# A new table of issue times for a fused conv, Fourier-attention and feed-forward kernel on one core

## The chip, the core and the metric

The kernel runs on one core of a Trainium2 chip. A core has a matrix engine (TensorE, PE in the profile; its weight loads are shown apart as PEld), a vector engine (VectorE, DVE), a scalar engine (ScalarE, ACT), a general engine (GpSimd, POOL) and a queue engine (SyncE, SP) that here only issues DMA transfers. Each works through its own list of instructions in order, and they wait for each other by semaphores. SBUF is the working memory, PSUM the memory that TensorE writes its products to[...].

The metric is the time of one execution on the device in microseconds (us), lower being better.

## What is computed

The input is x of 64 images, 96 channels, 56 x 56 pixels, in float32. Two layers follow each other:

```python
# layer 0: inverted bottleneck with squeeze and excitation
out = silu(bn(conv1x1(x, 96 -> 192)))
out = channel_shuffle(shift_groups(out))            # by one pixel up, left, down, right
out = silu(bn(bn(depthwise3x3(out)) + bn(out * id_w)))
se  = sigmoid(grouped(relu(grouped(mean(out)))))    # one gate per channel
x   = silu(bn(conv1x1(out * se, 192 -> 96)) + x)

# layer 1: tokens t of 3136 pixels x 96 channels
def attn(t):                                        # a Fourier filter over the tokens
    X  = fft(relu(bn(t @ w1.T)), axis=1, norm='ortho')
    xr = relu(X.real * diag(r) - X.imag * diag(i) + rb)
    xi = relu(X.imag * diag(r) + X.real * diag(i) + ib)
    return bn(ifft(xr + 1j * xi).real @ w2.T)
t = t + attn(ln(t))
t = t + qlinear(relu(qlinear(ln(t), W1, b1)), W2, b2)   # inputs and weights rounded to fp8 e5m2, sums to fp16
```

## The kernel before

The work of an image is cut into 56 kinds of steps, most of them in several pieces: 7 pieces of x to load, 7 ea_mm steps and so on. A step is a Python function that issues a few instructions on one engine. There is no loop over images with a body: line 42 holds PERIOD and line 43 a table PLAN with one number for every piece of every kind, and at the end of the kernel one sort puts all pieces of all 64 images in one order:

```python
for _, b, k, i in sorted(
    (b * PERIOD + when, b, k, i)
    for b in range(NB)
    for k, step in enumerate(STEPS)
    for i, when in enumerate(PLAN[step.__name__])
):
    STEPS[k](b, i)
```

The numbers are only sort keys: nothing on the chip looks at a time. What they settle is the order in which each engine's instructions are issued, and with it which image's pieces stand between which others, and the order in which buffers are taken from their pools. About four images are in work at a time. While image b has its depthwise product, image b-1 has its Fourier product, and image b-2 its feed-forward part. Waits on data, on buffers and on shared PSUM banks are put in by the framework, following that order.

In the order of one image, with the engine and the line that the profile shows:

- **x_in** (SP, L175): 7 pieces of 8 image rows into the single buffer `xi`, two transfers of 48 channels each. A piece may overwrite its rows once the `pj_add` steps of the image before have read them.
- **ea_mm, eb_mm** (PE, L383, L400) with **ea_ev, eb_ev** (ACT, L388, L413): the expanding 1x1 product with the shift built into the window, 128 channels in `e_a` and 64 in `e_b`.
- **dw_mm** (PE, L446) with **dw_ev** (ACT, L456): the depthwise product of the 128 channels as 32 x 32 diagonal products, in two halves of three steps of 96 products each. A half takes all four tiles of the pool `psb`; steps 0 to 2 are the first, 3 to 5 the second half. dw_ev 0 to 3 and 4 to 7 read the tiles out.
- **lt** (DVE, L466 and L468) and **ls** (ACT, L471): the nine taps of the other 64 channels, and their silu.
- **se1, se2** (PE, ACT, DVE), ending in se2_pw (DVE, L517), which makes the gated projection weight `pw`.
- **pj_mm** (PE, L532, L537), **pj_add** (DVE, L543), **pj_ev** (ACT, L549): the projection in two halves, the addition of x, and the silu into one of three buffers `t`.
- **c_mm, c_sq, c_v, c_pow, sp** (PE, ACT, DVE, POOL): the first layernorm's sums. sp_ev ends with a small transfer on SP (L612).
- **w1_mm, w1_ev** (PE L626, DVE L638); **f1_mm, f1_ev** (PE L653, ACT L665); **f2_mm** (PE L680, L690): the attention's first product and the Fourier transform in two stages. f2_mm has six groups of frequency rows, each in one tile of `psa`, of which there are two; a tile takes two PSUM banks.
- For each f2 group i: **f2_u** 2i and 2i+1 (ACT, L705) read the tile's first 56 columns per row into the two halves of `ue`; **f2_s** 2i and 2i+1 (DVE, L721 and L724) read its other 56 columns and each half of `ue`, two instructions per step; **f2_r** i (ACT, L728) and **f2_p** i (DVE, L734) make the filtered values.
- **w2_mm, w2_ev** (PE L745 and L757, ACT L775); **i1_mm, i1_ev** (PE L786, ACT L797); **i2_mm, i2_ev** (PE L808, DVE L821): output product and inverse transform. All of w2, i1, i2, w1, f1 and f2 take turns at the two `psa` tiles. i1_mm has three steps of 128 products of 56 columns each; the first two stand next to each other behind pj_mm 3, which belongs to the next image.
- **n, x_mm, x_ev** (PE, ACT, DVE, POOL), then **h_mm, h_ev, h_b, h_q** (PE L865, ACT L870, DVE L875, ACT L881), 21 steps each, and **o_mm, o_ev, o_b, o_f, o_st** (PE L887, ACT L892, DVE L897, POOL L903, SP L909), 7 each: the second layernorm, the quantized feed-forward part, the last addition and the store.

The pool `psb` has four tiles of one PSUM bank and hands them out in turn, so a step that takes a tile waits for the one that took it four tiles ago to be read out. The order on PE around the depthwise product of image b is, before the change: f2 1 and 0 (of b-1), dw 0, 1, 2 (of b), f2 2, h 6, h 8, h 7 (of b-2), f2 3, dw 3, 4, 5, f2 4, h 9, o 1, se1, f2 5, h 10, se2, h 12, h 11, w2 0, w2 1, and then pj 0 of b.

## Time and profile before

| | us |
|---|---|
| median of 3 runs | 7470.06 |
| lowest and highest | 7461.43, 7473.81 |
| the profiled execution | 7463.64 |
| its span, first to last instruction | 7461.9 |
| busy: PE, DVE, ACT, POOL | 7176.9, 4829.5, 4654.4, 1513.6 |
| granted TensorE clock | 0.991 |

The span is 1.7 us short of the profiled execution's own time. The costliest groups on PE are the depthwise product (1033.2 us busy, 36864 products of 498 ns, which overlap), the Fourier product f1 (688.9), w1 (676.2), ea (429.6) and eb (415.3). On DVE it is the taps of the 64 channels (971.5, 512 of 1898 ns), on ACT the 1344 casts h_q (739.0) and the 1344 casts h_ev (697.2). DMA engines are busy about a tenth of the time.

Busy times are sums over overlapping work, and the end of a product on PE is modelled; so start times are the better measure of PE's progress. "issue" as the releaser of a wait means that the engine waited for nothing that the profile shows.

### The profile page before, as it was taken

How to read it: one execution, taken by the hardware profiler on the slowest of the kernel's cores; microseconds unless marked ns; L12 is line 12 of the kernel's file. 1: busy time of each engine (PE TensorE's matmuls, PEld its weight loads, DVE VectorE, ACT ScalarE, POOL GpSimd, SP SyncE). 2: the span in 40 equal slices, each digit the busy share in tenths (PEclk: the TensorE clock that was granted, in tenths of full speed). 3: DMA queues.
4: the chain of work that ended last, by engine and by line, in shares of the span. 5: the costliest groups of instructions: out<-in, count | busy, mean ns of one | idle time of the engine just before them, and what ended most of it. 6: DMA issues, size and time to landing. Idle time of an engine off the chain costs nothing.

```text
span 7461.9 us, 383252 instructions
## 1 busy us (share of the span) xinstructions
PE 7176.9 (96%) x177666; PEld 5259.2 (70%) x177666; DVE 4829.5 (65%) x8795; ACT 4654.4 (62%) x9806; POOL 1513.6 (20%) x1360
## 2 busy tenths in 40 slices
PE   7999999999999999999999999999999999999997
PEld 4777777777777776777777777777777777777775
DVE  5666666666666666666666666666666666666664
ACT  3566666666665666656656666666566566665665
POOL 0221212212212122122121221221212212212112
PEclk9999999999999999999999999999999999999998
DMA  1010110110101101101011011010110110101100
GB/s 48 20 27 18 29 27 19 29 24 21 28 17 29 27 19 28 24 22 28 17 29 27 19 28 25 22 28 18 29 27 19 29 26 20 29 21 26 28 20 21
DMA packets 424331, 185.32 MB, mean 25 GB/s; under 512 B 378785, under 2 KB 422041, under 8 KB 422473
## 3 DMA queue, kind: packets, MB, share of 16 engines
q1 hardware_dynamic: 420970, 155.82, 9.1%
q8 instruction: 1392, 22.81, 1.3%
q10 hardware_dynamic: 1264, 3.48, 0.1%
q14 instruction: 209, 1.71, 0.1%
q0 software_dynamic: 496, 1.50, 0.1%
HBM read 82.80 MB, written 77.07 MB: 21 GB/s over the span
## 4 chain that ended last, share of the span: by engine, by line
PE 85%; ACT 6%; DVE 6%; issue 3%; DMA 0%; POOL 0%; POOLq 0%; SPq 0%; ACTq 0%
PE psa L653 9%; PE psa L626 9%; PE ps_d L446 8%; PE ps_eb L400 5%; PE ps_ea L383 5%; PE psa L808 5%; PE ps_pj L532 5%; PE ps_c L557 5%; PE psa L745 5%; PE ps_n L557 5%; PE psa L786 5%; PE psa L680 4%; PE ps_h L865 4%; PE ps_o L887 3%; DVE s L721 3%
## 5 line engine op out<-in xcount | busy, mean ns | idle before, releaser
L903 POOL TENSOR_TENSOR o<-t,o 112x448 f32<-112x448 f32 x448 | 613.9, 1370 | 3694.7 <-DMA out_dram<-o 1710.0
L446 PE MATMUL ps_d<-e_a,diag 32*32 32x392 f32 x36864 | 1033.2, 498 | 0.7 <-ACT d L456 0.7
L468 DVE SCALAR_TENSOR_TENSOR d_last<-e_b,taps,d_last 128x1568 f32<-128x1568 f32 x512 | 971.5, 1898 | 7.1
L875 DVE TENSOR_SCALAR y<-y,qb 128x448 f16<-128x448 f16 x1344 | 479.8, 365 | 683.9 <-ACT y L870 676.7
L568 DVE TENSOR_REDUCE v<-sq 112x4 f32<-112x384 f32 x896 | 491.3, 548 | 662.7 <-ACT sq L564 662.1
L446 PEld LDWEIGHTS ps_d<-e_a,diag 32*32 32x32 f32 x36864 | 673.6, 103 | 288.9 <-issue 40.0
L870 ACT CAST y<-ps_h 128x448 f16<-128x448 f32 x1344 | 697.2, 540 | 213.1 <-PE ps_h L865 209.5
L837 POOL TENSOR_TENSOR rs<-v,mhalf 112x4 f32<-112x4 f32 x448 | 490.3, 1099 | 1453.9 <-DVE v L569 1453.9
L881 ACT CAST h<-y 128x448 fp8e5<-128x448 f16 x1344 | 739.0, 571 | 3.0 <-DVE y L875 3.0
L653 PEld LDWEIGHTS psa<-f_tab,buf_h 128*56 128x56 f32 x24576 | 655.4, 131 | 77.8 <-DVE v L569 42.5
L626 PEld LDWEIGHTS psa<-w1c,t 112*64 112x64 f32 x14336 | 604.0, 137 | 141.4 <-DVE v L569 45.4
L653 PE MATMUL psa<-f_tab,buf_h 128*56 128x58 f32 x24576 | 688.9, 216 | 0.0
L626 PE MATMUL psa<-w1c,t 112*64 112x96 f32 x14336 | 676.2, 249 | 2.9 <-DMA t<-dev_t 1.4
L586 POOL TENSOR_TENSOR rs<-v,mhalf 112x4 f32<-112x4 f32 x448 | 447.6, 1012 | 763.6 <-DVE v L569 763.5
L638 DVE SCALAR_TENSOR_TENSOR buf_h<-psa,rs_full 128x768 f32<-128x768 f32 (+1 forms) x512 | 435.4, 851 | 137.4 <-PE psa L626 129.5
L543 DVE TENSOR_TENSOR ps_pj<-ps_pj,x 112x392 f32<-112x392 f32 x512 | 260.6, 566 | 404.5 <-PE ps_pj L537 392.3
L728 ACT ACTIVATE s<-s 128x896 f32<-128x896 f32 (+2 forms) x384 | 334.4, 887 | 288.8 <-DVE s L721 288.8
L388 ACT ACTIVATE e_a<-ps_ea 128x448 f32<-128x448 f32 x448 | 244.9, 547 | 412.5 <-PE ps_ea L383 412.5
L564 ACT ACTIVATE sq<-ps_n 112x384 f32<-112x384 f32 x448 | 214.1, 495 | 436.1 <-PE ps_n L557 434.8
L734 DVE SCALAR_TENSOR_TENSOR buf_h<-ue,s 128x448 f32<-128x448 f32 (+2 forms) x768 | 406.8, 580 | 109.4 <-ACT s L728 109.4
L549 ACT ACTIVATE t<-ps_pj,pjbn_b 112x392 f32<-112x392 f32 x512 | 281.4, 620 | 284.5 <-DVE ps_pj L543 284.5
L786 PE MATMUL psa<-inv_tab,buf_g 112*32 112x56 f32 x24576 | 350.5, 214 | 110.5 <-issue 108.8
(175 smaller groups left out, 13024.5 us busy)
## 6 DMA issues: line engine op xcount, KB each, us to landing
x<-in_x SPq DMA_DIRECT2D x896, 84.0 KB, 3.2
out_dram<-o SPq DMA_DIRECT2D x896, 84.0 KB, 2.2
l_tab<-in_tab_l ACTq DMA_DIRECT2D x1, 1624.0 KB
r_tab<-in_tab_r ACTq DMA_DIRECT2D x1, 1568.0 KB
t<-dev_t SPq DMA_DIRECT2D x64, 7.0 KB, 2.1
t<-dev_t SPq DMA_DIRECT2D x64, 5.2 KB
ex_row_p<-in_expand_row POOLq DMA_DIRECT2D x1, 336.0 KB, 4.5
s_p<-in_bn POOLq DMA_DIRECT2D x1, 288.0 KB, 3.8
```

What stands on the lines that cost most here:

```text
L446: nc.tensor.matmul(pss[r][j * 32 : j * 32 + 32], lhsT=diag[pr, tap, :], rhs=e_a[pr, r0 : r0 + PJ, dx : dx + HW], start=tap == 0, stop=tap ...
L468: nc.vector.scalar_tensor_tensor(d_last, win, w, d_last, ALU.mult, ALU.add)
L557: nc.tensor.matmul(cen[c0:c1, k, 0:C], lhsT=t_of(b)[:, n0 + c0 : n0 + c1], rhs=center, start=True, stop=True)
L568: nc.vector.tensor_reduce(v, sq, AX.X, ALU.add)
L626: nc.tensor.matmul(ps[hc * 64 : hc * 64 + 64, k, 0:C], lhsT=t[:, n0 : n0 + 64], rhs=w1c[:, hc * C : hc * C + C], start=True, stop=True,)
L653: nc.tensor.matmul(ps[r * 64 : r * 64 + HW, k, 0 : 2 * NK], lhsT=buf_h[:, n0 : n0 + HW], rhs=f_tab[:, r, :], start=True, stop=True,)
L786: nc.tensor.matmul(ps[p0 : p0 + 32, k, 0:HW], lhsT=u_v[:, oh * 48 + o, :], rhs=inv_tab[:, r, :], start=True, stop=True,)
L837: nc.gpsimd.tensor_tensor(rs, held.pop(("nv", b, g)), mhalf[0:CP, 0:4], ALU.pow)
L870: nc.scalar.copy(y16, held.pop(("h", b, i)))
L875: nc.vector.tensor_scalar(y16, y16, qb1[:, i % 3 : i % 3 + 1], 0.0, ALU.add, ALU.max)
L881: nc.scalar.copy(held["h8", b, j][:, m, :], held.pop(("y", b, i)), saturate=False)
L903: nc.gpsimd.tensor_tensor(o32, rows, o16, ALU.add)
```

## The change

Every number of PLAN and PERIOD (116.056, then 116.315) is replaced. No step function, no buffer and no other line differs: the same pieces with the same instructions are issued in another order. The rows of the diff that the prediction speaks of:

```diff
-    "x_in": (-142.751, -132.334, -138.890, -139.641, -151.208, -133.652, -137.370),
+    "x_in": (-162.051, -141.566, -142.305, -147.704, -149.731, -127.852, -144.579),
-    "dw_ev": (-67.184, -68.088, -65.354, -62.005, -53.949, -53.481, -53.376, -53.432),
+    "dw_ev": (-75.276, -74.363, -73.773, -71.247, -63.274, -62.310, -61.437, -59.461),
-    "ls": (-56.957,),
+    "ls": (-63.791,),
-    "c_mm": (-24.403, -20.404, -19.123, -17.297, -18.726, -9.644, -8.872),
+    "c_mm": (-31.436, -30.770, -31.175, -30.095, -27.535, -26.998, -26.407),
-    "f2_u": (39.991, 41.910, 38.664, 38.665, 56.185, 56.316, 56.071, 58.643, 62.858, 62.962, 66.464, 67.055),
-    "f2_s": (42.369, 43.646, 41.684, 42.524, 58.496, 59.412, 59.011, 59.603, 66.349, 66.780, 67.365, 69.133),
-    "f2_r": (44.699, 46.227, 59.499, 60.966, 71.228, 72.985),
-    "f2_p": (46.153, 47.154, 60.124, 60.967, 72.402, 74.345),
+    "f2_u": (36.232, 37.748, 35.978, 39.758, 48.352, 51.224, 45.857, 47.326, 55.183, 57.358, 59.477, 63.260),
+    "f2_s": (40.754, 40.796, 41.011, 41.830, 49.823, 52.099, 45.858, 50.177, 56.136, 57.359, 62.673, 66.022),
+    "f2_r": (40.797, 43.254, 52.791, 53.034, 64.718, 69.300),
+    "f2_p": (44.390, 44.463, 53.286, 53.767, 68.705, 72.198),
-    "i1_mm": (82.811, 83.639, 91.924),
+    "i1_mm": (78.634, 79.503, 87.989),
```

On PE the order stays close to what it was. Around the depthwise product it is now f2 0, h 3, f2 1, dw 0, 1, 2, f2 3, h 7, h 8, h 6, f2 2, dw 3, 4, 5, f2 4, f2 5, h 9, o 1, se1, h 10, se2, h 12, h 11, w2 0, w2 1, pj 0. The order on ACT between dw_ev 0 and w2_ev 0, before and after (h and o steps are of image b-2, dw, ls and se steps of b, f2 and w2 of b-1):

```
before: dw_ev 1, 0, 2, h_ev 6, 8, dw_ev 3, h_ev 7, f2_u 6, 4, h_q 6, f2_u 5, 7, ls, f2_r 2, 3, dw_ev 4, 5, 7, 6,
        f2_u 8, 9, se1_ev, o_ev 1, h_ev 9, h_q 8, f2_u 10, 11, h_q 7, h_ev 11, se2_th, h_ev 10, w2_ev 0
after:  dw_ev 0, 1, 2, f2_r 1, h_ev 6, 8, dw_ev 3, h_ev 7, f2_u 6, 7, 4, 5, h_q 6, 8, ls, f2_r 2, 3, dw_ev 4, 5, 6,
        f2_u 8, dw_ev 7, h_ev 9, f2_u 9, se1_ev, o_ev 1, f2_u 10, h_ev 10, f2_u 11, h_q 7, f2_r 4, h_ev 11, h_q 9,
        se2_th, w2_ev 0
```

On DVE the f2_s steps of the second pair of groups change from 4, 6, 5, 7 to 6, 4, 7, 5. On SP the order per image changes from x 4, o_st 5, o_st 0, x 0, 3, 2, 6, o_st 2, x 5, 1, o_st 1 to x 0, o_st 0, x 4, 3, 6, 2, 1, o_st 1, o_st 4, sp_ev 0, x 5, where the stores belong to an image three before that of the loads (o_st 5 and 0 of the old order to two other ones).

More of the change, by code (lines that the diff above doesn't have):

```diff
@@ L38 @@
 AT = {k: i for i, k in enumerate(ROWS)}
-PERIOD = 116.056
+PERIOD = 116.315
 PLAN = {
-    "x_in": (-142.751, -132.334, -138.890, -139.641, -151.208, -133.652, -137.370),
-    "ea_mm": (-127.116, -124.446, -119.920, -94.498, -104.745, -112.167, -106.964),
-    "ea_ev": (-125.252, -124.279, -119.721, -94.105, -94.974, -110.456, -105.960),
-    "eb_mm": (-110.852, -109.364, -102.468, -94.672, -100.705),
-    "eb_ev": (-109.889, -108.508, -98.175, -94.671, -100.704),
-    "dw_mm": (-77.186, -75.415, -71.686, -59.708, -58.836, -58.630),
-    "dw_ev": (-67.184, -68.088, -65.354, -62.005, -53.949, -53.481, -53.376, -53.432),
-    "lt": (-93.236, -91.843, -90.397, -86.333, -83.176, -78.618, -75.060, -71.072, -58.358),
-    "ls": (-56.957,),
-    "se1_mm": (-52.674,),
-    "se1_ev": (-52.590,),
-    "se2_mm": (-49.560,),
-    "se2_ev": (-47.764,),
-    "se2_th": (-46.882,),
-    "se2_pw": (-44.842,),
-    "pj_mm": (-44.604, -44.263, -36.259, -33.499),
-    "pj_add": (-41.623, -41.337, -40.573, -40.255, -32.468, -30.814, -32.509, -32.127),
-    "pj_ev": (-41.036, -40.637, -40.429, -36.736, -30.334, -29.230, -31.146, -29.797),
-    "c_mm": (-24.403, -20.404, -19.123, -17.297, -18.726, -9.644, -8.872),
-    "c_sq": (-23.198, -19.663, -17.391, -16.366, -11.963, -8.651, -8.871),
-    "c_v": (-21.831, -17.939, -17.390, -11.021, -10.842, -8.366, -8.657),
-    "c_pow": (-19.058, -12.292, -10.931, -8.952, -1.526, -3.948, -1.526),
-    "sp_v": (-8.951, -1.525),
-    "sp_mm": (-6.057, 0.802),
-    "sp_ev": (-5.461, 1.113),
-    "w1_mm": (1.423, -2.619, 3.588, 18.203, 8.943, 12.171, 13.999, 16.535),
-    "w1_ev": (3.273, -0.045, 7.600, 20.920, 11.591, 14.999, 15.957, 19.212),
-    "f1_mm": (21.608, 26.248, 24.638, 31.810, 32.559, 32.004),
-    "f1_ev": (25.169, 25.895, 30.841, 28.844, 27.556, 26.595, 32.009, 32.411, 36.910, 36.732, 36.699, 35.929),
-    "f2_mm": (37.220, 36.994, 44.528, 54.196, 60.721, 63.959),
-    "f2_u": (39.991, 41.910, 38.664, 38.665, 56.185, 56.316, 56.071, 58.643, 62.858, 62.962, 66.464, 67.055),
-    "f2_s": (42.369, 43.646, 41.684, 42.524, 58.496, 59.412, 59.011, 59.603, 66.349, 66.780, 67.365, 69.133),
-    "f2_r": (44.699, 46.227, 59.499, 60.966, 71.228, 72.985),
-    "f2_p": (46.153, 47.154, 60.124, 60.967, 72.402, 74.345),
-    "w2_mm": (70.359, 71.061, 73.352, 79.154),
-    "w2_ev": (70.421, 73.788, 79.483, 82.773),
-    "i1_mm": (82.811, 83.639, 91.924),
-    "i1_ev": (86.931, 93.317, 99.344),
-    "i2_mm": (102.107, 101.737, 110.644, 111.766),
-    "i2_ev": (106.004, 107.037, 104.651, 104.395, 113.248, 110.645, 115.503, 113.393),
-    "n_mm": (109.042, 108.523, 116.336, 120.505, 126.604, 126.539, 137.374),
-    "n_sq": (109.105, 109.021, 116.337, 120.506, 127.174, 126.540, 137.375),
-    "n_v": (109.642, 109.022, 116.338, 120.507, 127.975, 126.902, 138.122),
-    "n_pow": (110.809, 110.170, 116.496, 122.658, 132.126, 129.135, 139.318),
-    "n_x": (112.520, 110.693, 119.248, 123.053, 133.298, 130.929, 139.362),
-    "x_mm": (113.125, 114.113, 121.321, 126.216, 135.244, 138.382, 142.002),
-    "x_ev": (114.896, 115.709, 126.025, 126.217, 137.926, 142.365, 142.302),
@@ new lines @@
+    "x_in": (-162.051, -141.566, -142.305, -147.704, -149.731, -127.852, -144.579),
+    "ea_mm": (-137.812, -138.766, -127.145, -89.430, -97.733, -111.642, -106.253),
+    "ea_ev": (-135.094, -135.727, -126.517, -84.394, -93.721, -111.545, -104.661),
+    "eb_mm": (-115.802, -120.129, -109.842, -102.415, -108.473),
+    "eb_ev": (-111.833, -116.221, -108.303, -102.404, -105.700),
+    "dw_mm": (-76.334, -76.333, -76.332, -65.377, -64.292, -64.065),
+    "dw_ev": (-75.276, -74.363, -73.773, -71.247, -63.274, -62.310, -61.437, -59.461),
@@ new lines @@
+    "lt": (-98.494, -96.392, -95.603, -88.519, -87.554, -85.563, -82.511, -76.163, -74.006),
+    "ls": (-63.791,),
+    "se1_mm": (-59.375,),
+    "se1_ev": (-58.823,),
+    "se2_mm": (-58.487,),
+    "se2_ev": (-51.685,),
+    "se2_th": (-49.080,),
+    "se2_pw": (-49.031,),
+    "pj_mm": (-46.907, -46.770, -39.776, -38.214),
+    "pj_add": (-46.414, -46.480, -46.303, -45.926, -36.420, -35.642, -35.383, -35.834),
+    "pj_ev": (-44.579, -44.088, -42.412, -41.675, -36.419, -34.237, -33.877, -33.743),
@@ new lines @@
+    "c_mm": (-31.436, -30.770, -31.175, -30.095, -27.535, -26.998, -26.407),
+    "c_sq": (-30.893, -30.081, -28.190, -27.946, -25.511, -26.729, -24.086),
+    "c_v": (-30.249, -28.487, -27.216, -25.783, -23.070, -24.232, -21.605),
+    "c_pow": (-28.779, -21.220, -25.415, -24.356, -20.189, -23.395, -9.184),
+    "sp_v": (-20.657, -9.105),
+    "sp_mm": (-16.179, -7.327),
+    "sp_ev": (-14.695, -0.897),
+    "w1_mm": (0.527, -6.007, -2.422, 8.757, 3.678, 7.621, 13.788, 13.807),
+    "w1_ev": (4.695, -0.847, -2.421, 11.306, 5.010, 10.078, 15.828, 14.929),
@@ new lines @@
+    "f1_mm": (20.887, 18.211, 16.353, 22.113, 25.063, 24.097),
+    "f1_ev": (22.512, 22.072, 20.634, 20.909, 16.354, 19.684, 23.039, 23.663, 29.327, 28.458, 27.295, 25.063),
+    "f2_mm": (31.295, 32.252, 47.080, 41.210, 52.876, 55.792),
+    "f2_u": (36.232, 37.748, 35.978, 39.758, 48.352, 51.224, 45.857, 47.326, 55.183, 57.358, 59.477, 63.260),
+    "f2_s": (40.754, 40.796, 41.011, 41.830, 49.823, 52.099, 45.858, 50.177, 56.136, 57.359, 62.673, 66.022),
+    "f2_r": (40.797, 43.254, 52.791, 53.034, 64.718, 69.300),
@@ new lines @@
+    "f2_p": (44.390, 44.463, 53.286, 53.767, 68.705, 72.198),
+    "w2_mm": (65.362, 69.052, 70.502, 74.617),
+    "w2_ev": (67.901, 69.923, 78.367, 78.466),
+    "i1_mm": (78.634, 79.503, 87.989),
+    "i1_ev": (85.994, 87.591, 88.690),
+    "i2_mm": (93.044, 93.367, 101.562, 100.521),
+    "i2_ev": (96.799, 93.389, 96.982, 100.266, 111.406, 109.631, 107.480, 103.660),
+    "n_mm": (96.952, 99.575, 108.486, 116.587, 121.041, 122.075, 127.209),
+    "n_sq": (99.791, 100.349, 108.487, 117.309, 121.042, 122.726, 128.090),
@@ L91 @@
+    "n_v": (101.981, 103.127, 109.950, 117.332, 122.940, 123.624, 129.985),
+    "n_pow": (101.982, 103.583, 112.829, 119.179, 122.941, 123.625, 129.986),
+    "n_x": (105.486, 105.615, 113.313, 120.038, 125.778, 125.828, 132.761),
+    "x_mm": (106.100, 106.737, 115.863, 120.681, 125.990, 132.998, 133.784),
+    "x_ev": (106.881, 107.368, 115.976, 121.004, 126.865, 132.999, 134.355),
     "h_mm": (
-        144.408, 144.539, 142.955, 151.653, 146.123, 151.741, 165.593, 167.081, 167.021, 179.037, 181.701, 184.163,
@@ L93 @@
-        183.315, 191.401, 194.122, 202.572, 203.025, 214.978, 205.482, 214.132, 209.133,
+        136.544, 135.201, 136.984, 147.819, 144.613, 140.473, 159.661, 157.770, 158.449, 172.175, 173.774, 178.994,
+        177.277, 189.872, 189.465, 197.605, 199.164, 206.608, 200.687, 210.643, 205.066,
     ),
     "h_ev": (
-        146.457, 147.163, 146.728, 153.132, 153.156, 154.262, 168.465, 171.753, 169.119, 180.037, 185.733, 184.280,
-        187.040, 192.972, 195.243, 203.531, 205.107, 216.376, 208.878, 222.205, 212.052,
+        137.275, 137.145, 138.242, 147.961, 147.833, 147.527, 159.834, 162.046, 160.395, 173.266, 179.005, 181.613,
@@ L98 @@
+        184.463, 191.247, 191.928, 199.351, 199.788, 208.901, 200.878, 212.968, 205.403,
     ),
     "h_b": (
-        146.899, 148.834, 148.614, 154.505, 157.941, 159.836, 170.515, 176.287, 174.097, 185.812, 187.639, 185.918,
-        191.781, 195.030, 198.861, 204.123, 206.545, 220.428, 209.152, 226.370, 218.475,
+        137.276, 141.744, 141.117, 153.242, 154.679, 148.788, 161.282, 173.396, 162.133, 182.903, 186.070, 184.378,
+        188.999, 195.975, 191.954, 201.844, 202.120, 210.978, 202.978, 215.917, 208.435,
@@ L102 @@
     ),
     "h_q": (
-        149.384, 151.139, 150.029, 159.215, 163.340, 163.159, 172.257, 183.329, 182.397, 187.024, 188.763, 189.403,
-        196.328, 198.478, 200.406, 208.755, 210.002, 221.499, 217.314, 229.791, 224.579,
-    ),
-    "o_mm": (153.028, 179.101, 192.712, 203.850, 207.474, 223.800, 230.382),
-    "o_ev": (154.015, 179.621, 193.552, 207.958, 209.955, 223.824, 232.254),
-    "o_b": (167.276, 193.254, 201.506, 209.696, 210.604, 235.187, 237.499),
-    "o_f": (171.766, 199.519, 206.356, 219.602, 231.322, 259.139, 253.186),
@@ L111 @@
-    "o_st": (197.792, 218.616, 214.282, 229.895, 257.122, 313.688, 263.438),
+        140.919, 141.749, 144.251, 155.904, 156.312, 156.480, 168.059, 179.758, 168.312, 182.908, 186.075, 186.567,
+        191.342, 197.228, 195.477, 205.150, 206.001, 211.207, 209.270, 222.571, 223.802,
+    ),
+    "o_mm": (146.182, 172.743, 190.451, 200.773, 200.074, 212.764, 232.857),
+    "o_ev": (146.312, 174.620, 191.421, 200.998, 200.479, 216.027, 234.615),
+    "o_b": (153.419, 184.679, 196.437, 223.964, 201.880, 232.421, 251.929),
@@ L112 @@
+    "o_f": (177.091, 191.561, 197.796, 234.593, 212.317, 240.011, 266.796),
+    "o_st": (192.867, 211.246, 229.825, 253.850, 214.262, 288.749, 273.012),
 }
```

## The prediction

> **What bounds the kernel now.** I read the head of the page, then the waits, then one period of the timeline on PE, ACT, DVE and SP.

> ```profile
> span 7461.9 us, 383252 instructions
> PE 7176.9 (96%) x177666; PEld 5259.2 (70%) x177666; DVE 4829.5 (65%) x8795; ACT 4654.4 (62%) x9806; POOL 1513.6 (20%) x1360
> q8 instruction: 1392, 22.81, 1.3%
> ```
> PE is busy 96% of the span. The other engines are a third idle over a period, so they matter only where PE waits for one of them. The third line is the fetch of a program: 1392 pieces of 16 KB, [...]which is what PE's 355,332 products and weight loads need: 21.75 per image.

> From one dw step 0 to the next (the first product on L446) the median is 114.5 us. The two PE waits that repeat per image:

> ```profile
> PE psa L786 <- issue: 108.8, 68, 2.2
> PE psa L745 <- DVE ue L724: 50.8, 64, 1.7
> ```
> The first (L786 = i1_mm) names no releaser, the second is w2 step 0 waiting for the second half of f2_s. The timeline of image 26's depthwise stage shows the second one, and the order that the change rearranges (start, duration, engine, line):

> ```profile
> 3016.07 1.75 PE L680 MATMUL psa<-l_tab,buf_g 128*64 128x112 f32 x32
> 3017.76 7.98 PE L446 MATMUL ps_d<-e_a,diag 32*32 32x392 f32 x288
> 3025.66 1.56 PE L690 MATMUL psa<-l_tab,buf_g 128*64 128x112 f32 x28
> 3031.92 1.29 PE L745 MATMUL psa<-w2a,buf_h 128*64 128x96 f32 x26 [0.83 <-DVE ue L724]
> ...
> 3017.23 0.54 ACT L870 CAST y<-ps_h 128x448 f16<-128x448 f32 x1
> 3017.88 1.34 ACT L705 ACTIVATE ue<-psa,fa 128x448 f32<-128x448 f32 x2
> 3019.56 1.35 ACT L705 ACTIVATE ue<-psa,fa 128x448 f32<-128x448 f32 x2
> 3020.79 1.61 ACT L471 ACTIVATE d_last<-d_last,mid_b 128x1568 f32<-128x1568 f32 x1
> 3024.98 0.95 ACT L728 ACTIVATE s<-s 128x896 f32<-128x896 f32 x1 [0.36 <-DVE s L721]
> 3025.84 0.57 ACT L456 ACTIVATE d<-ps_d,mid_b 128x392 f32<-128x392 f32 x1
> ...
> 3020.33 0.68 DVE L721 SCALAR_TENSOR_TENSOR s<-psa,fa,ue 128x448 f32<-128x448 f32 x1 [0.89 <-ACT ue L705]
> 3029.38 0.62 DVE L721 SCALAR_TENSOR_TENSOR s<-psa,fb,ue 128x392 f32<-128x392 f32 x1 [1.33 <-ACT ue L705]
> 3031.24 0.63 DVE L724 SCALAR_TENSOR_TENSOR ue<-psa,fb,ue 128x392 f32<-128x392 f32 x1
> ```
> Three things to see. ACT ends h_ev 7 (L870) at 3017.77, and dw step 3 on PE, begun at 3017.76, has its fourth product 53 ns later: no slack. ACT takes up dw_ev 4 (L456) at 3025.84, where the last product of dw ended at 3025.73: no slack either. And DVE starts the f2_s of a group only when *both* f2_u of that group are done (33 ns after the second ends, though the first ended 0.6 to 1.1 us earlier and DVE stands idle), although a half reads only its own half of ue.

> [...]

> **The change part by part.** Only the order of issue changes. Sorting both tables gives the same 106 PE steps per image. I count from dw step 0 = 0 (3005.84 before), with start-to-start times of the trace: f2_u 0.62 (0.56 for 7 rows, 0.48 for 5), a pair on f2_s 1.32 (1.40 to its end), f2_r 0.86, dw_ev 0.57, ls 1.60, h_ev 0.43, h_q 0.46, f2_p 1.1.

> *1. f2_r 1 before h_ev 6 on ACT.* The new ACT order after dw step 2 is dw_ev 0, 1, 2, f2_r 1, h_ev 6, 8, dw_ev 3, h_ev 7. Before, f2_r 1 came ahead of the dw_ev. dw step 2 ends at 7.94, f2_r 1 starts 1.72 later and holds 0.86, so h_ev 6 starts at 10.52 (before 9.96) and h_ev 7 ends at 12.49. The four tiles of dw step 3 take the PSUM slots of dw_ev 3 and the three h_ev, so its products go on at 12.55 instead of 11.99: **+0.56**. dw step 5 ends at 20.46.

> *2. f2_u and f2_s interleaved.* Before, every f2_u was issued ahead of its group's f2_s. Now the order for the second pair of groups is u6, s6, u7, u4, s4, s7, u5, s5, and for the last two u8, s8, u9, s9 and u10, s10, u11, s11. [...] ACT takes its work in order, so everything behind waits too:
> - u6 12.38 to 13.08, s6 13.11 to 14.51, u7 14.56, u4 15.18 to 15.90, s4 15.93 to 17.33, u5 17.38; s7 and s5 run on to 19.97.
> - behind u5: h_q 6 18.00, h_q 8 18.46, ls 18.92, f2_r 2 20.52, f2_r 3 21.38, and only then dw_ev 4 at 22.24. dw was over at 20.46: ACT is 1.7 us late, where it was 0.1 late.
> - dw_ev 4, 5, 6, then u8 23.95 to 24.64 (now before dw_ev 7, which saves 0.57), s8 to 25.96, u9 26.01 to 26.70, s9 to 28.02. w2 step 0 needs the buffer: 28.07, before 26.08: **+1.99** including the 0.56.
> - se1_ev, o_ev 1, u10 27.13, s10 to 28.97, u11 29.02 to 29.60, s11 to 30.67. w2 step 1 starts at 30.72, before 28.36. The gate's pw (se2_th 31.6, se2_pw to 32.6) is still ahead of pj step 0 at 32.99, before 30.63: **+2.36** from here on.

> PE has nothing else to do there: its products between dw and w2 (f2 4 and 5, h, o, se) take 5.3 us and are all issued ahead of w2.

> *3. pj to i1.* f2_p 5 now stands behind pj_add on DVE. pj_add ends 39.4, f2_p 5 40.2, w2 step 3 is wanted at 40.8; h 14, h 13 and o 2 come ahead of it and o 2 waits 0.1 for pj_ev 2. **+0.1**.

> *4. Gaps between kinds of steps on PE.* The trace gives every kind of change the same gap each time: from the last product of ea to any other kind 0.47 us, eb 0.42 (0.14 after its small step), h 0.28 to 0.29, o 0.28, w1 or n or c 0.18, to its own kind 0.03 to 0.2. Counting both orders (c to c 3 then 5, w1 to ea 2 then 0, x to x 0 then 2, h to w2 2 then 1, and so on), the new order saves 0.20 us per image. 0.13 of it lies before the w2 wait and is lost there: **-0.07**.

> *5. Loads of x.* A stall in i1 comes where two fetches follow within 1.7 us; the resumed product lies 3.2 to 4.3 us (median 3.6) after the previous block's first. All stalls of this kind (each step's time above its quickest tenth over images 8 to 55: i1, and the c and o steps behind it) are 3.4 us per image. x pieces 3, 2 and 6 are issued 0.7 to 2.7 us after i1 begins:

> ```profile
> 3050.79 0.31 SPq L175 DMA_DIRECT2D x<-in_x  x1
> ...
> 7293.28 0.79 PE L786 MATMUL psa<-inv_tab,buf_g 112*32 112x56 f32 x45 [1.35 <-issue]
> ```
> The second line is image 62, at whose i1 no x is left to load (the last x is issued at 7183.3): it stalls 1.35 on this page, against 2.08 for image 25. So most of the stall isn't the loads. On SP the order becomes x 0, o_st 0, x 4, 3, 6, 2, 1: x 3 is now behind the last pj_add of its rows and fires about 2.3 us after i1 begins instead of 0.7. These are 14 loads as before, they only move past o_st 2 and sp_ev 0; x 1 still lands some 9 us before ea step 1, x 5 some 3 us before eb step 1. I take **-0.2**; bounds: 0, if the fetch doesn't feel them, and -0.6, if every stall fell to 3.2.

> The rest (c steps ahead of i1 step 2, w1, n, x, f1) I followed step by step in the same way: each finds its slot and its input 0.3 us or more before PE asks. The tightest are w1_ev 6 before f1, and f1_ev 8 before f2 step 0 (0.4 and 0.6).

> Sum: 2.36 + 0.1 - 0.07 - 0.2 = 2.2 us per image. It acts in the 63 periods in which one image's dw meets the f2 of the one before: +138 us on the profiled execution's 7463.6, 7602. The median shown lies 6 above that execution, so I say 7605. Filling and draining I leave as they are (63 periods of 114.5 leave about 250 us for both; their chains have the same steps).

> **The rivals.** *(a) The waits run one way only*: a f2_u needn't wait for the f2_s in front of it. Then ls is done by 17.4 and ACT is ready when dw ends. Part 1 stays (+0.56), w2 step 0 gains 0.3 and step 1 gives it back: +0.6 + 0.1 - 0.27, about +25 us, 7490. For it: before never issues an f2_u behind an f2_s of its group, so the trace doesn't show the reverse wait. Against it: the 33 ns rule holds in all three groups in which DVE stood waiting[...].
> *(b) Faster, by the fetch*: place L786 and the c and o steps behind it, price at most 0.6 per image by fewer collisions plus 0.2 of gaps, 0.8 x 63 = 50 us, 7415. It decides only if the dw stage costs under 0.8 per image, that is if (a) holds and the slot wait of part 1 is hidden as well. For it: the stalls are the largest wait. Against it: image 62.
> *(c) The loads don't move*: SP sends when pj_add lets it, whatever the table says. Then -0.2 becomes 0: 7618.
> *(d) The lateness compounds*: ACT, late by 1.7, also delays pj_ev and the h chain, another 0.7 per image: 7650.

> **How the numbers follow.** Forecast with (c), 7560 to 7640: 0.67. (d): 0.10. (a): 0.12, a third of it within 0.2%. (b): 0.11. The range that leaves out two tenths reaches from 7530 to 7655. A measurement of this kernel tells about 0.2% (15 us) from no change: faster 0.11, same 0.05, slower 0.84.

> **What would show it.** Right: f2_u 7 and f2_u 5 start just after an f2_s ends; dw_ev 4 starts 1.5 us or more after the last product of dw; the wait on L745 grows from 0.8 to about 2 us per image and a wait appears inside dw step 3 (some 0.6 us); the period is near 116.7. Wrong: f2_u 7 starting beside s6, an L745 wait that shrinks, or an L786 stall well below 1 us.

## The result and the profile after

The new table is slower: 7650.10 us (median of 4 runs, 7645.42 to 7655.18) beside 7465.75 for the kernel before (4 runs), a ratio of 1.0246 with a 95% interval of 1.0228 to 1.0264. That is 184 us, or 2.93 us for each of the 63 periods. The profiled execution took 7655.18 us.

The head of its page, and the waits on PE (in all, times, longest, us):

```profile
span 7653.4 us, 383102 instructions
PE 7322.0 (96%) x177666; PEld 5365.9 (70%) x177666; DVE 4895.7 (64%) x8795; ACT 4669.8 (61%) x9806; POOL 1722.1 (23%) x1360
```
```profile
PE psa L786 <- issue: 100.6, 81, 2.0
PE ps_se L493 <- ACT red L485: 66.6, 64, 1.3
...
PE ps_se L478 <- ACT d L456: 35.9, 67, 0.9
...
PE psa L745 <- DVE ue L724: 0.6, 1, 0.6
```
PE executes the same instructions and is busy 145 us longer (7322.0 beside 7176.9): its products themselves got slower somewhere. The granted clock fell from 0.991 to 0.974. The wait on L745 (w2), 50.8 us before, is gone; in its place PE waits in se1 (L478) and se2 (L493), which stand ahead of w2 in PE's queue and want dw_ev 7 and se1_ev from a late ACT. A reader who looks only at L745 would think that w2 no longer waits.

Image 26, the same stretch as in the prediction (start, duration; dw step 0 is at 3077.58):

```profile
3089.88 0.78 ACT L705 ACTIVATE ue<-psa,fa 128x448 f32<-128x448 f32 x1
3092.13 1.34 ACT L705 ACTIVATE ue<-psa,fa 128x448 f32<-128x448 f32 x2 [1.47 <-DVE ue L724]
3094.94 0.72 ACT L705 ACTIVATE ue<-psa,fa 128x448 f32<-128x448 f32 x1 [1.47 <-DVE ue L724]
3095.57 1.02 ACT L881 CAST h<-y 128x448 fp8e5<-128x448 f16 x2
3096.49 1.60 ACT L471 ACTIVATE d_last<-d_last,mid_b 128x1568 f32<-128x1568 f32 x1
...
3099.77 0.57 ACT L456 ACTIVATE d<-ps_d,mid_b 128x392 f32<-128x392 f32 x1
...
3091.41 0.68 DVE L724 SCALAR_TENSOR_TENSOR ue<-psa,fa,ue 128x448 f32<-128x448 f32 x1
...
3094.22 0.69 DVE L724 SCALAR_TENSOR_TENSOR ue<-psa,fa,ue 128x448 f32<-128x448 f32 x1
...
3098.23 1.56 PE L690 MATMUL psa<-l_tab,buf_g 128*64 128x112 f32 x28
...
3105.54 1.53 PE L745 MATMUL psa<-w2a,buf_h 128*64 128x96 f32 x32
...
3110.57 2.90 PE L532 MATMUL ps_pj<-d,pw 32*112 32x392 f32 x32
```
f2_u 7 starts 14.55 us after dw step 0, 40 ns after f2_s 6 ended at 3092.09, and f2_u 5 at 17.36, 30 ns after f2_s 4: here an f2_u waits for the f2_s in front of it. The prediction counts on that; it was an estimate of mine, which no trace had shown. dw_ev 4 starts at 22.19 where dw was over at 20.7, w2 step 0 at 27.96 and pj step 0 (L532) at 32.99. The prediction had 14.56, 17.38, 22.24, 28.07 and 32.99.

Image 26 is one of the few whose w2 runs at its usual speed; image 25 is the commoner kind. Its PE timeline, and the clock in three stretches of it (stretch, length, busy and count of PE, PEld, DVE, ACT, POOL, PEclk, DMA):

```profile
2983.21 0.36 PE L865 MATMUL ps_h<-xq,q 96*128 96x448 fp8e5 x1
2984.62 0.60 PE L493 MATMUL ps_se<-red,ep_w 24*32 24x1 f32 x32 [1.05 <-ACT red L485]
...
2986.32 2.82 PE L745 MATMUL psa<-w2a,buf_h 128*64 128x96 f32 x32
2989.08 1.55 PE L757 MATMUL psa<-w2b,buf_h 64*64 64x96 f32 x32
2990.56 1.57 PE L745 MATMUL psa<-w2a,buf_h 128*64 128x96 f32 x32
```
```profile
2980.40:2983.80 3.40, 2.38 (x31) 1.26 (x25) 2.48 (x6) 3.04 (x11) 0.00 (x0) 1.00 0.00 0
2983.80:2990.60 6.80, 5.98 (x104) 4.77 (x104) 4.70 (x12) 4.87 (x11) 0.00 (x0) 0.50 0.01 2
2990.60:2994.00 3.40, 3.40 (x83) 2.75 (x84) 2.45 (x4) 2.71 (x5) 1.98 (x1) 0.99 0.03 5
```
The same 32 products of w2 take 2.82 us here and 1.53 in image 26 and in step 1. For 6.8 us the clock is at 0.50, and the fall comes in the pause itself, before se2 (L493) starts. In 57 of the 60 images 2 to 61, w2 step 0 runs in this slow way, each time at the lower clock; before the change, in none. I had not foreseen it.

### The profile page after: what moved, and what is told of

It reads as the page before. It is cut to its first block, busy times and chain, and to the rows that moved or that the text cites. A ratio compares the mean times of both kernels' runs of the same rounds, so it can differ in the third digit from the quotient of the medians.

```text
span 7653.4 us, 383102 instructions
## 1 busy us (share of the span) xinstructions
PE 7322.0 (96%) x177666; PEld 5365.9 (70%) x177666; DVE 4895.7 (64%) x8795; ACT 4669.8 (61%) x9806; POOL 1722.1 (23%) x1360
## 4 chain that ended last, share of the span: by engine, by line
PE 81%; ACT 12%; DVE 4%; issue 2%; DMA 0%; POOL 0%; POOLq 0%; SPq 0%; DVEq 0%; ACTq 0%
PE psa L653 9%; PE psa L626 8%; PE ps_d L446 7%; PE psa L745 5%; PE ps_ea L383 5%; PE ps_eb L400 5%; PE psa L808 5%; PE ps_pj L532 5%; PE psa L786 4%; PE ps_n L557 4%; PE ps_c L557 4%; PE ps_h L865 4%; ACT d L456 3%; PE ps_o L887 3%; ACT ue L705 3%; PE psa L757 3%
## 5 line engine op out<-in xcount | busy, mean ns | idle before, releaser
L903 POOL TENSOR_TENSOR o<-t,o 112x448 f32<-112x448 f32 x448 | 823.0, 1837 | 3756.1 <-DVE o L897 3140.0
L446 PE MATMUL ps_d<-e_a,diag 32*32 32x392 f32 x36864 | 1062.6, 498 | 0.8 <-ACT d L456 0.7
L468 DVE SCALAR_TENSOR_TENSOR d_last<-e_b,taps,d_last 128x1568 f32<-128x1568 f32 x512 | 1003.2, 1959 | 7.1
L446 PEld LDWEIGHTS ps_d<-e_a,diag 32*32 32x32 f32 x36864 | 698.9, 103 | 293.5 <-issue 26.7
L875 DVE TENSOR_SCALAR y<-y,qb 128x448 f16<-128x448 f16 x1344 | 497.4, 382 | 634.1 <-ACT y L870 627.3
L870 ACT CAST y<-ps_h 128x448 f16<-128x448 f32 x1344 | 695.0, 539 | 321.2 <-PE ps_h L865 318.9
L837 POOL TENSOR_TENSOR rs<-v,mhalf 112x4 f32<-112x4 f32 x448 | 448.9, 1011 | 1336.6 <-DVE v L569 1336.5
L586 POOL TENSOR_TENSOR rs<-v,mhalf 112x4 f32<-112x4 f32 x448 | 451.1, 1015 | 801.2 <-PE ps_c L557 437.0
L859 ACT CAST xq<-ps_x 96x448 fp8e5<-96x448 f32 x448 | 224.7, 531 | 624.8 <-PE ps_x L852 624.8
L665 ACT COPY buf_g<-psa 128x464 f32<-128x464 f32 x768 | 402.1, 550 | 175.7 <-PE psa L653 175.7
L705 ACT ACTIVATE ue<-psa,fa 128x448 f32<-128x448 f32 (+1 forms) x512 | 341.2, 692 | 245.3 <-DVE ue L724 245.3
L745 PEld LDWEIGHTS psa<-w2a,buf_h 128*48 128x48 f32 (+1 forms) x7424 | 384.8, 152 | 113.9 <-issue 63.5
```

The costliest lines, as they stand in the source:

```text
L446: nc.tensor.matmul(pss[r][j * 32 : j * 32 + 32], lhsT=diag[pr, tap, :], rhs=e_a[pr, r0 : r0 + PJ, dx : dx + HW], start=tap == 0, stop=tap ...
L468: nc.vector.scalar_tensor_tensor(d_last, win, w, d_last, ALU.mult, ALU.add)
L705: nc.scalar.activation(held["ue", b, i][:, q, 0:n, :], held["f2", b, i][:, 0:n, 0:HW], AF.Identity, bias=par[:, 2 + q : 3 + q], scale=par[ ...
L745: nc.tensor.matmul(ps[c0:c1, u, k, 0:C], lhsT=pq_a[:, AT[k1], c0:c1], rhs=w2a, start=k == 0, stop=False, skip_group_check=True,)
L870: nc.scalar.copy(y16, held.pop(("h", b, i)))
L875: nc.vector.tensor_scalar(y16, y16, qb1[:, i % 3 : i % 3 + 1], 0.0, ALU.add, ALU.max)
```

## The experiments

Starts on PE, taken from the traces: medians over images 8 to 55, in us after dw step 0, and the mean period (the first product of dw to the next image's). The right column counts the images 2 to 61 whose w2 step 0 is slow, that is, whose products start over more than 2.3 us (normally 2.1).

```
kernel                    dw end   w2 0    w2 1    pj 0    period   slow w2
before                    19.99    26.11   28.39   30.67   114.69    0
after                     20.42    28.38   32.11   34.44   117.62   57
e1  after, u first        20.43    26.18   28.62   30.90   114.24   23
e2  before, mixed         19.92    28.01   31.51   33.94   117.63   32
e3  before, r 1 moved     20.45    26.53   28.80   31.08   114.74   not counted
e4  after, filler         20.43    28.40   30.73   33.00   116.19    2
e12 last version          19.90    25.95   28.23   30.51   112.79   not counted
```
The experiments ran on other chips than the first two rows. There the kernel before has a median of 7450 to 7454, up to 0.2% less than above, so I compare times by their ratio to the runs of before on the same chip, and starts and waits by the traces.

**The order of f2.** My theory: the turns of f2_u and f2_s in the table of after make ACT late, and the slow clock follows from the pause. *e1* takes the turns out of after:

```diff
# in after; f2_u 7, 5, 9, 11
-    "f2_u": (36.232, 37.748, 35.978, 39.758, 48.352, 51.224, 45.857, 47.326, 55.183, 57.358, 59.477, 63.260),
+    "f2_u": (36.232, 37.748, 35.978, 39.758, 48.352, 49.000, 45.857, 45.8575, 55.183, 55.184, 59.477, 62.000),
```

> The kernel after, with one difference: f2_u 7, 5, 9 and 11 are issued ahead of the first f2_s of their group. Theory O (the alternation of f2_u and f2_s costs it, and the fall of the granted clock in w2 step 0 follows from the long pause that it makes): without it dw_ev 4 is on time, w2 step 0 starts near 26.4 us after dw step 0 (28.3 in after), w2 runs at the full clock, pj step 0 starts near 31.0 (34.6 in after), and the time falls to 7400 to 7450, below the kernel before. Rival T (something else in the new table costs it, the order of f2 only shows it): 7600 to 7650.

Measured: 7444.72 us, ratio 0.9996 (0.9987 to 1.0004). Four numbers of the table, moved, give all of the 2.46% back. On ACT (image 26, dw step 0 at 2995.13):

```profile
3007.44 2.62 ACT L705 ACTIVATE ue<-psa,fa 128x448 f32<-128x448 f32 x4
...
3010.80 1.68 ACT L471 ACTIVATE d_last<-d_last,mid_b 128x1568 f32<-128x1568 f32 x1
...
3015.54 0.59 ACT L456 ACTIVATE d<-ps_d,mid_b 128x392 f32<-128x392 f32 x1 [0.17 <-PE ps_d L446]
```
The four f2_u run back to back, and now ACT waits for PE at dw_ev 4, not PE for ACT. The expected w2 at full clock came in 37 of 60 images only. The others cost 0.66 us per image on average at pj step 0 (31.42 beside 30.76, means), some 40 us of the 7445; what empties its pause follows under "The clock".

*e2* puts the turns into the kernel before:

```diff
# in before; the last four groups
-    "f2_u": (39.991, 41.910, 38.664, 38.665, 56.185, 56.316, 56.071, 58.643, 62.858, 62.962, 66.464, 67.055),
-    "f2_s": (42.369, 43.646, 41.684, 42.524, 58.496, 59.412, 59.011, 59.603, 66.349, 66.780, 67.365, 69.133),
+    "f2_u": (39.991, 41.910, 38.664, 38.665, 58.420, 58.450, 56.071, 58.410, 62.858, 62.962, 66.464, 67.055),
+    "f2_s": (42.369, 43.646, 41.684, 42.524, 58.430, 58.460, 58.400, 58.440, 62.900, 66.400, 66.500, 69.133),
```

> The kernel before, with only the f2_u and f2_s of the last four groups issued in turn as in the kernel after. Theory O: dw_ev 4 comes 1.5 us after the end of dw, w2 step 0 starts 1.8 us later than before, pj step 0 2.4 us later at the full clock: 7465 + 63 x 2.4 = 7615; where the clock falls in w2 as it does in after, up to 1.3 us per image more: 7610 to 7700. Rival A (a f2_u needn't wait for the f2_s in front of it): 7460 to 7490.

Measured: 7660.51 us, ratio 1.0282 (1.0269 to 1.0295). The waits on ACT name the cause, a group that the kernel before doesn't have (in after it is 268.7 us in 255 waits):

```profile
ACT ue L705 <- DVE ue L724: 360.0, 256, 2.0
```
256 waits are 4 per image, the four f2_u that now follow an f2_s. Added or taken away, the turns decide. Rival A has fallen. What makes an f2_u wait isn't separated by a run: it shares with the f2_s both the PSUM banks of psa and the tile ue, though not the same half of it. That ue as a whole is held is the less likely of the two, since this kernel does not hold the tile xi as a whole: in the kernel before, 16 loads of x were in flight over the whole of a pj_add that reads other rows of it.

**The clock.** My theory, an estimate: the clock falls because TensorE has too little to do in the pause. *e4* keeps all of after and gives it something to do there. The products read data that lies ready and write columns that nobody reads:

```diff
# in after, se2_mm, ahead of its products
+        full = psb.tile([128, 128], F32, tag="psb", name="ps_se2")
+        ps = full[:, 0:NG]
+        for k in range(8):
+            for c0 in (0, 64):
+                nc.tensor.matmul(full[c0 : c0 + 64, 16:128], lhsT=g_v[:, k, c0 : c0 + 64], rhs=l_tab[:, k, :], start=True, stop=True)
```

> The kernel after, with 16 products more per image (f2's shape, 0.9 us together) into unused columns of the tile of se2, issued just ahead of se2, where TensorE only waits. Their results aren't used. Clock theory C (the clock falls to half in w2[...]): w2 step 0 runs at the full clock again, w2 step 0 to pj step 0 falls from 6.2 to about 4.7 us, and the kernel gets faster by up to 63 x 1.3 = 80 us though it does more work: 7570 to 7620. Rival (the slow w2 has another cause, such as the data or the fetch of instructions): same or slower, 7640 to 7700.

Measured: 7559.28 us, ratio 1.0146 (1.0133 to 1.0159), so 1.0% less than after (75 us by the ratios; the periods of the two traces, 117.62 and 116.19, give 90), with more work. Image 25 again, on PE, and the clock in stretches of 3.4 us:

```profile
2934.64 1.75 PE L494 MATMUL ps_se<-l_tab,buf_g 128*64 128x112 f32 x32
...
2937.37 1.53 PE L755 MATMUL psa<-w2a,buf_h 128*64 128x96 f32 x32
```
```profile
2931.60:2935.00 3.40, 2.60 (x37) 1.56 (x35) 2.49 (x6) 3.03 (x11) 0.00 (x0) 1.00 0.02 5
2935.00:2938.40 3.40, 3.40 (x92) 2.85 (x90) 2.34 (x6) 2.52 (x7) 0.00 (x0) 1.00 0.00 0
```
The filler (L494) takes 1.75 us, not the 0.9 that I had expected: the 16 float32 products that the source adds per image have 32 records on TensorE. (Elsewhere in this text the products are counted by records.) It pushes w2 step 0 to 28.40 also where after starts it at 27.96, and yet w2 runs at 1.53 and pj step 0 comes 1.4 us earlier than in after. The slow images fall from 57 to 2. So in this kernel the slow w2 is the clock (1.00 over these 32 products, 0.50 over those of after), and the fall of the clock a matter of how little TensorE had to do ahead of it.

The turns are not the only thing in the new table that empties the pause. f2 step 5 has changed its place on TensorE, here in before (image 26) and in after (image 25):

```profile
3028.56 1.18 PE L680 MATMUL psa<-l_tab,buf_g 128*64 128x112 f32 x20
```
```profile
2979.58 1.13 PE L680 MATMUL psa<-l_tab,buf_g 128*64 128x112 f32 x20
```
In before it stands behind se1 (L478, from 3028.02) and fills the stretch ahead of se2; in after and e1 it is over before h 9 and se1. It shows when the columns of data that the products of a stretch read are counted (112 for a product of f2, 1 for one of se2). In the emptiest 3.41 us (the length of 41 of the 73 low stretches in the clock's record of after) that begin between the end of dw and w2 step 0, there are in the median 3588 columns in before (no slow w2), 3154 in e4 (2), 2806 in e1 (23), 2706 in e2 (32) and 502 in after (57). The time for which PE counts as busy doesn't give this order: 2.58 us in before and 2.93 in e1. A run that moves only f2 step 5 is missing, so its share isn't shown.

**f2_r 1 and the slots of dw step 3.** *e3* moves only f2_r 1 in the kernel before:

```diff
# in before
-    "f2_r": (44.699, 46.227, ...
-    "f2_p": (46.153, 47.154, ...
+    "f2_r": (44.699, 51.000, ...
+    "f2_p": (46.153, 51.100, ...
```

> The kernel before, with only f2_r 1 (and f2_p 1, which needs it) moved behind dw_ev 2, so ahead of h_ev 6 on ACT as in after. Slot theory: h_ev 7 ends 0.56 us later, the fourth product of dw step 3 starts at 12.55 instead of 11.99, and 63 x 0.56 = 35 us come on top: 7500. Rival (slack further on takes it up): under 10 us.

Measured: 7477.36 us, ratio 1.0033 (1.0021 to 1.0045), 25 us; dw ends 0.46 us later and pj step 0 starts 0.41 later. The mechanism is right, the size three quarters of the expected. The reverse comes with e11.

**Loads of x, and the c steps.** After without its delay should be ahead of before, so something outside the dw stage gained: from pj step 0 to the end of the period the two profiles differ by 0.86 us. *e5* moves only the loads, *e6* only the c steps, *e9* both:

```diff
# e5, in before
-    "x_in": (-142.751, -132.334, -138.890, -139.641, -151.208, -133.652, -137.370),
+    "x_in": (-156.556, -139.356, -139.456, -139.556, -150.056, -121.056, -139.656),
# e6, in before
-    "c_mm": (-24.403, -20.404, -19.123, -17.297, ...
-    "c_sq": (-23.198, -19.663, -17.391, -16.366, ...
-    "c_v": (-21.831, -17.939, -17.390, -11.021, ...
+    "c_mm": (-24.403, -24.390, -24.400, -24.380, ...
+    "c_sq": (-23.198, -22.800, -22.400, -22.300, ...
+    "c_v": (-22.900, -22.500, -22.200, -22.000, ...
```

> The kernel before, with only the issue of x changed to the order of after: x 0, o_st 0, x 4, then the other pieces behind the last pj_add, x 5 much later. X theory (the gain outside the depthwise stage comes from loads that no longer meet the fetch of instructions in i1 and c): 0.2 to 0.7 us per image less, 13 to 45 us, 7408 to 7440, with the c steps losing their stalls. Rival (the gain comes from the order of the c steps): within 10 us of before.

> The kernel before, with only the c steps put as in after: c 0, 2, 1 and 3 ahead of i1 step 2 (before: only c 0), and their c_sq and c_v with them. C theory (a c step has few instructions for its time, so four of them between two steps of i1 give the fetch time to catch up): 0.5 to 0.8 us per image less, 30 to 50 us, 7400 to 7425. Rival (the gain comes from the loads of x): within 10 us of before.

> The kernel before with both the issue of x and the c steps of after, and nothing else. Alone they gave 9 and 24 us. If they are all of what the new table gains outside the depthwise stage and add up: 33 us, 7408 to 7428. If both remove the same stalls: about 24 us, 7420 to 7438. If there is more in them together, as the 0.86 us per image of the two profiles would have it: 54 us, 7390 to 7405.

Measured: the loads 7440.77 us, 0.9988 (0.9981 to 0.9994), 9 us; the c steps 7430.24 us, 0.9968 (0.9957 to 0.9978), 24 us; both 7421.66 us, 0.9961 (0.9947 to 0.9975), 29 us. Both gain, and both gain less than I had expected (13 to 45 us and 30 to 50 us); the loads stay within the 10 us that their rival allowed. Whether the two add up isn't decided: 7421.66 lies in the range for adding up and in that for the same stalls. With four c steps between two steps of i1, c step 1 takes 0.59 us where it took 0.86 (from its first product to its last, means). Of the 0.86 us per image they explain about 0.5 (29 us over 63 periods). What the rest is, I haven't separated; part of it is the chip, since the traces from the other chips give 0.7 (82.92 us from pj step 0 on in e4, 83.61 in e3).

**The fetch in i1.** In the kernel before, 1392 packets of 16 KB on queue q8 go with PE's 355,332 products and weight loads, 255 to a packet. Counted in the order in which these run, 61 of the 64 breaks of 0.9 us or more between the starts of two products of i1 lie whole multiples of 256 apart. From these counts I estimate a packet at one block of 256 instructions, as much as one step of i1 has (128 products and 128 weight loads). If two such blocks in 3.1 us are too much, something else between them should end the stall. *e7* moves pj step 3 there, *e10* also w2_ev 3:

```diff
# e7, in before
-    "pj_mm": (-44.604, -44.263, -36.259, -33.499),
+    "pj_mm": (-44.604, -44.263, -36.259, -32.800),
# e10, besides
-    "w2_ev": (70.421, 73.788, 79.483, 82.773),
+    "w2_ev": (70.421, 73.788, 79.483, 80.000),
```

> The kernel before, with pj step 3 (24 products, 1.6 us or more) moved from ahead of i1 step 0 to between i1 steps 0 and 1. Fetch theory (256 instructions in 1.57 us are asked for faster than they come; two such blocks in a row stall 1.7 us): the stall of the pair falls to 0.5 us or less, 1.2 us per image less, 7453 - 75 = 7380, range 7345 to 7425. Rival (the stall has a cause in i1 itself, such as its buffer): within 15 us of before.

Measured: 7442.25 us, 0.9988 (0.9982 to 0.9995). 9 us where 75 were expected: a miss. The waits on PE in e7 show that it isn't the theory of the stall that fails:

```profile
PE ps_o L887 <- ACT y L870: 50.7, 62, 1.3
...
PE psa L786 <- ACT buf_g L775: 40.5, 63, 1.6
...
PE psa L786 <- issue: 10.5, 11, 1.7
```
"issue" on L786 fell from 108.8 to 10.5. But i1 step 0, now 2.1 us earlier, waits for w2_ev 3 (L775), and the o steps behind it wait for tiles that h_ev has to read out: on ACT it stands behind pj_ev, which now runs 2.6 us later. The gain turned into two new waits.

That the stall is the fetch is read from the packets of q8 in the kernel before. Every one of the 63 stalls of L786 over 0.8 us ends 1.2 to 1.7 us after the end of such a packet, and no two packets start less than 3.2 us apart, while i1 uses up a block in 1.6 us.

> The kernel of e7_b_pj3, with w2_ev 3 also moved ahead of h_q 12 and 13 on ACT. Theory (the fetch stall of 1.6 us did go in e7, and was replaced by a wait of i1 step 0 for w2_ev 3, 0.7 us, and by later waits for tiles, 1.0 us): the first of the two goes, 63 x 0.7 = 43 us less than e7, 7385 to 7410. Rival (the gain is eaten by the tiles of psb whatever i1 step 0 does): 7430 to 7445.

Measured: 7400.54 us, 0.9934 (0.9922 to 0.9947), some 40 us less than e7 by the ratios. One of the two new waits, that for L775, is gone, and the other stays:

```profile
PE ps_o L887 <- ACT y L870: 49.7, 62, 1.3
```

**A version that beats both.** *e8* is e1 with pj step 3 between i1 steps 0 and 1 (its number -38.214 becomes -37.300) and e4's filler at half its size (`range(4)`). *e11* also moves f2_r 1 ahead of the dw_ev (its number 43.254 becomes 41.831, that of dw_ev 0 -74.400). *e12* also exchanges the numbers of h steps 6 and 7 on TensorE (157.770 and 159.661).

> The kernel after, with f2_u ahead of f2_s as in e1_u_first, pj step 3 between i1 steps 0 and 1, and 8 products without use (0.43 us) ahead of se2 against the fall of the clock in w2. If the three gains add up: 7445 - 75 (fetch) - up to 40 (the clock in a quarter of the images) = 7330 to 7370. If the clock isn't held by 8 products: 7370 to 7400.

Measured: 7382.05 us, 0.9908 (0.9894 to 0.9922). "issue" on L796, as i1 is called there, falls to 11.7 us in all, and no w2 step 0 is slow. So the clock is held (0.995 granted), although the time lies in the range that I had given for the case that it isn't (7370 to 7400). The filler takes 0.9 us, not 0.43, and fills PE up to w2, which starts 0.3 us later than in e1; this can account for some 18 us of what is missing from the sum. The run changes three things at once, and what each is worth here isn't separated.

> The kernel of e8_a_best, with f2_r 1 also moved ahead of the dw_ev on ACT. Slot theory: dw step 3 no longer waits, all that follows to pj comes 0.45 us earlier, 63 x 0.45 = 28 us, 7345 to 7365. Rival (the wait only moves to w2): 7375 to 7385.

Measured: 7373.07 us, 0.9896 (0.9882 to 0.9909). 9 us, near the rival's range, but not for the rival's reason: dw itself ends only 0.14 us earlier. In image 26, h_ev 6 starts at 10.50, where e8 has 10.48, because h step 6 is now the last of three h steps on PE and ends at 10.46, while ACT asks for it first.

> The kernel of e11_a_best2, with h step 6 also ahead of h 8 and 7 on TensorE, as it was before the change; in after it runs last of the three while ACT reads it first. Order theory (in after, h_ev 6 is late for two reasons, f2_r 1 ahead of it and its product running last, so that taking f2_r 1 away gave 0.13 us where 0.45 were expected): h_ev 6 starts at 10.0 instead of 10.5, dw step 3 no longer waits, 0.4 us per image less from there on, 63 x 0.4 = 25 us, 7340 to 7355. Rival (w2 step 0 waits for f2_s 9 anyway): 7365 to 7375.

Measured: 7353.13 us, 0.9868 (0.9852 to 0.9884). h_ev 6 starts at 9.97, dw ends at 19.90 as in the kernel before, and pj step 0 comes at 30.51. This is 97 us less than before on the same chip and, by the ratios, 3.7% less than after (some 280 us). PE is busy for 98% of its span.

## Why the prediction was right, and where not

The sign, the place and the mechanism of the delay were right. The size came out 45 us short of 7650, which lies above the 7560 to 7640 that I thought likeliest, and that it is no further off is luck: two terms were wrong in opposite directions. In the means of the traces, pj step 0 comes 3.79 us later than before, where I had 2.36, and the rest of the period is 0.86 us shorter, where I had 0.17 (+0.1 - 0.07 - 0.2). The first error alone would have made it some 90 us, the second takes some 44 of them back.

- **Part 2, the turns of f2_u and f2_s: right.** Removed (e1) or added (e2), they carry the change. The sum to pj step 0 was +2.36, and image 26, whose w2 ran at the full clock, has pj step 0 at 32.99 as forecast; so has e4, with 33.00 (median). That e4 agrees to the hundredth is partly chance, since its filler and se2, not f2_s 9, set the start of its w2 (28.40 beside the forecast 28.07). What the sum left out is how TensorE runs *after* the pause: from w2 step 0 to pj step 0 I took 4.92 us, and after needs 6.23 (mean), e4 4.66. This is the term that failed: I priced the products behind the pause as in the kernel before, and they cost 1.2 to 1.4 us more per image, 75 to 90 us. The clock's record of after has 73 low stretches, all at 0.50. But for two in the draining they are 3.413 us (41) or 6.827 us (30) long, and all begin on one grid of 3.413 us, to within 12 ns. The sentence "PE has nothing else to do there" was in the prediction; the question what that does to the clock wasn't.
- **Part 1, f2_r 1: the delay right, its cause only half.** 0.56 was forecast; dw ends 0.43 later in after, 0.46 in e3. But in after either of two changes gives most of it, f2_r 1 ahead of h_ev 6 on ACT or h step 6 behind h 7 and 8 on PE. Taking the first away gave 0.14, the second the remaining 0.38. I had the PE order in front of me and priced only the ACT side.
- **Part 5 and "the rest": too small.** The loads were put at -0.2 and gave -0.14 (9 us over 63 periods, e5). The c steps ahead of i1 step 2 I had looked at for slots and inputs, not for fetches; they gave -0.38 (24 us, e6). Both together gave 29 us (e9), so some 0.4 of the 0.86 us stays open.
- **Part 3, +0.1, was 0**: pj step 0 to i1 step 0 is 13.61 us in both profiles. **Part 4, -0.07**, is too small to be told from what remains.
- **What would show it**: f2_u 7 and 5 and dw_ev 4 came as described, and dw ended 0.43 later. The L745 wait didn't grow but vanished, which I had named as a sign of being wrong. It was a bad sign: the late ACT had first stopped se1 and se2, ahead of w2 on PE. The profile books the wait on the instruction of PE's queue that meets it first (66.6 and 35.9 us on L493 and L478, 0.6 on L745). The period was 117.62, not 116.7.
- **The rivals**: (a) fell with e2. (b) needed it. (c) fell with e5, narrowly (the interval ends at 0.9994). (d), at 7650, has the right time for the wrong reason: with the clock held up nothing compounds (from pj step 0 on, e4 needs 82.92 us, less than the 83.92 of the kernel before).

## What to carry to other kernels

Where ACT and DVE read the same tile of psa here, the order of issue was a dependence in both directions (an f2_s started 33 ns after the f2_u ahead of it, an f2_u 30 and 40 ns after the f2_s ahead of it); try all reads of one engine ahead of the other's rather than in turn, above all on an engine that others wait for (e1 has a ratio of 0.9996 beside the 1.0246 of after). When a change opens a pause on TensorE, look in the trace whether the products *behind* the pause run at a lower clock, as here (2.82 us beside 1.53 for w2's 32), and add that to its price, or put real or even idle products into it (e4, 57 slow images to 2); and count what the new order takes out of the stretch ahead of it. When a stall goes, look at once at what the instruction behind it needs, since here 75 us of a removed stall became 9 until the next input was moved as well.
